# One ring of double PSUM banks for scores and products, layer 0's v bias moved to ScalarE, token sums in two bursts

## The chip, the cores and the metric

The kernel runs on one core of a Trainium2 chip. The metric is the device time of one execution in microseconds; the kernel before has a median of 4040.7 us over three runs (4039.68 to 4045.5). Five engines work side by side, each in its own order of instructions: TensorE (PE in the profile; its weight loads are shown apart as PEld), VectorE (DVE), ScalarE (ACT), GpSimd (POOL) and SyncE (SP, which issues DMA). TensorE writes its products to PSUM[...], from where ScalarE or VectorE must read them before the bank can be used again.

## The reference

Two attention layers over x of shape (4, 32, 32, 768): 4 images, 1024 tokens each, 768 channels. Each layer adds its result to its input:

```python
x = x + _L0_conv_ref(_gn(x), Wq, bq, Wk, bk, Wv, bv, Wp, bp, rel_h, rel_w)
x = x + _L1_conv_ref(_gn(x), w_qkv, b_qkv, w_pool_q, ..., w_proj, b_proj)
```

_gn normalizes over 32 groups of channels. Layer 0 is attention with 12 heads of 64 channels and decomposed relative positions:

```python
q, k, v = heads(x @ Wq + bq), heads(x @ Wk + bk), heads(x @ Wv + bv)
attn = einsum('bqd,bkd->bqk', q, k) / sqrt(64)
attn = softmax(attn + rel_bias_h[:, :, :, :, None] + rel_bias_w[:, :, :, None, :])
return (attn @ v) @ Wp + bp
```

Layer 1 does the same after a depthwise 3x3 convolution and a layer norm over the 64 channels of a head on each of q, k and v, and adds its q to the attention's result before the projection.

The rows of a softmax sum to one, so the v bias bv of layer 0 may be added after the weighted sum: attn @ (x Wv + bv) = attn @ (x Wv) + bv. It may also be moved behind the projection, as the constant bv @ Wp + bp.

## The kernel before

**Work.** The kernel goes through 8 stages (an image and a layer; two images at a time), each of 6 pairs of heads: 48 pairs. A pair has 1024 queries in 2 chunks of 512 (QC) and 8 tiles of 128 keys (NKT).

**Attention of a pair (attend).** For a chunk, 2 groups of 4 key tiles. A score tile is 128 keys x 512 queries for both heads of the pair, in 2 PSUM banks: q times k for each head (line 669), and the position bias, added by a product with a matrix of ones (line 671). ScalarE takes the exponential of both banks into the tile e (line 676), VectorE adds e into acc (lines 682, 684), and TensorE multiplies v with e into the bank av (line 690). After the last group ScalarE copies av (line 632). The sums of the softmax follow while the next chunk is under way: a product of acc with ones into the bank z (sums, line 639), logarithm and exponential on ScalarE as a reciprocal, one Newton step and the product on VectorE (result, lines 654 to 661). These late parts are taken out of the list `rest`, one at each of four places of a chunk (more).

**The other products.** While a pair attends, TensorE makes the next pair's q, k and v. In layer 1: six products (padded, "qkv"), three centrings for the layer norm (centre, "ln_c", two banks each), four transposes back (back, "ln_t"). In layer 0, after the first two pairs, a Strassen scheme with seven products of quarters (sevens): first half into the banks m4m2 and m3m5, second half into m1m6 and m7. It works on sums of quarters of the tokens, which mix_tokens makes with five VectorE instructions (line 234) for each stage. In both layers: products with the position tables (positions, "rel", 2 banks one after the other), from which ScalarE, VectorE and a DMA by GpSimd make the bias (split, line 544). Finally each stage is projected (project, line 723), 12 products for a stage, laid beside the first pair of a later stage.

**PSUM.** Three pools: ps_s, two score tiles of 2 banks each; ps_av, 1 bank; ps_m, a ring of three single banks for all other products. A tile of a pool goes to the place of the tile that many places before it, and its first matmul waits until that tile's readers are done.

**Layer 0's v bias.** In the first image of each layer, project makes the product of the projection's weights and the v bias for each of 6 output blocks (pbias, lines 709 to 714; in layer 1 it is the layer norm's bias), adds the projection's bias and keeps it for all images. The projection's eviction on VectorE (line 723) adds it.

**Order.** The order on TensorE, VectorE, ScalarE and GpSimd is written out by hand: attend yields 16 steps for each pair, and the dictionary `events` says which pieces are emitted at each step. Of 16 steps, a group of four score tiles comes before steps 0, 4, 8 and 12, and the value products of the group before steps 2, 6, 10 and 14. For the stage that follows a layer 1 stage, the quarters' sums come at steps 0 to 4 of the pair before it, and the first Strassen product at step 4.

Of the kernel before, what the change touches and what calls it, by code (L numbers as in the profile page):

```python
# [9 lines left out]
F32 = mybir.dt.float32  # L10
F32R = mybir.dt.float32r
I32 = mybir.dt.int32
AF = mybir.ActivationFunctionType
ALU = mybir.AluOpType
AX = mybir.AxisListType
PSUM = bass.MemoryType.PSUM
# [29 lines left out]
def two_layers(ctx: ExitStack, tc: tile.TileContext, keep, x_in, wqkv, wproj, rels, windows, vrow, small, const, onehot, picks, out):  # L46
# [25 lines left out]
    work = pool("work", 2)  # L72
    one = pool("one", 1)
    stat = pool("stat", 3)
    ps_s = pool("ps_s", 2, space=PSUM)
    ps_av = pool("ps_av", 1, space=PSUM)
    ps_m = pool("ps_m", 3, space=PSUM)

    def bank(name):
        return ps_m.tile([P, 512], F32, tag="bank", name=name)  # L80

    def halves(ps, a, b, start=True, stop=True, **kw):

# [17 lines left out]
    def col(c, lo=0, hi=P):  # L101
        return sm[lo:hi, c : c + 1]
# [134 lines left out]
    def group_norm(stage):  # L237

        xn = xns[stage]
        st = stat.tile([P, NC * 2, 6], F32, tag="bn", name="bn", bufs=1)  # L240
        for n in range(NC):
            for h in range(2):
                nc.vector.bn_stats(st[:, 2 * n + h, :], xn[:, n, h * HALF : (h + 1) * HALF])
            if n in (1, 3):
                yield
        mv = stat.tile([P, 2], F32, tag="mv", name="mv")
        nc.vector.bn_aggr(mv, st.rearrange("p a b -> p (a b)"))
        yield
        yield
        group = cst[:, GROUP : GROUP + P]  # L250
        ps = bank("gn_mean")
        nc.tensor.matmul(ps[:, 0:1], group, mv[:, 0:1], start=True, stop=True)
        mean = stat.tile([P, 1], F32, tag="gmean", name="gmean")
        nc.vector.tensor_copy(mean, ps[:, 0:1])
        d = stat.tile([P, 1], F32, tag="gd", name="gd")
        nc.vector.tensor_sub(d, mv[:, 0:1], mean)
        nc.vector.scalar_tensor_tensor(d, d, d, mv[:, 1:2], ALU.mult, ALU.add)
        yield
        yield
        ps = bank("gn_var")  # L260
        nc.tensor.matmul(ps[:, 0:1], group, d, start=True, stop=True)
        v = stat.tile([P, 1], F32, tag="gv", name="gv")
        nc.vector.tensor_scalar(v, ps[:, 0:1], EPS, None, ALU.add)
        yield
        r = rsqrt(v, 1, "gn")
        yield
        for n in range(NC):
            nc.vector.tensor_scalar(xn[:, n, :], xn[:, n, :], mean, r, ALU.subtract, ALU.mult)  # L268
            if n % 2:
                yield  # L270
# [7 lines left out]
    sk = fixed.tile([P, NSMALL], F32, tag="sk", name="sk")  # L278
    nc.vector.tensor_scalar(sk, sm, SCALE, None, ALU.mult)

    pbias = fixed.tile([P, 2, NC], F32, tag="pbias", name="pbias")

    ones = fixed.tile([P, T], F32R, tag="ones", name="ones")
    plain = one.tile([P, T], F32, tag="whole", name="plain")
# [8 lines left out]
    class Pair:  # L293
# [15 lines left out]
        def sevens(self, s, second):  # L309

            xn = xns[self.b, self.layer]
            x11, x12, x21, x22 = (xn[:, n : n + 3, h : h + HALF] for n in (0, 3) for h in (0, HALF))

            def m(ps, at, x, more=False):

                w = weights[self.i, s, at // 2][:, 3 * (at % 2) : 3 * (at % 2) + 3, :]  # L320
                for t in range(4 if s else 1):
                    for n in range(3):
                        flags = dict(start=not (t or n or more), stop=n == 2, skip_group_check=True)
                        if s:
                            tokens = slice(t * P, (t + 1) * P)
                            halves(ps[:, tokens], x[:, n, tokens], w[:, n, :], **flags)
                        else:
                            halves(ps, w[:, n, :], x[:, n, :], **flags)

            add = lambda to, x, y, op=ALU.add: nc.vector.tensor_tensor(to, x, y, op)  # L330
            u, w = terms
            if not second:
                self.banks = b1, b2 = bank("m4m2"), bank("m3m5")
                m(b1, 0, x21)
                nc.scalar.copy(u, b1)
                m(b2, 1, x12)
                used((self.i, s, 0))
                add(u, u, b2)
                m(b1, 2, x11, more=True)
                add(w, u, b1, ALU.subtract)  # L340
                self.put(s, 1, 0, b1)
                m(b2, 3, x22, more=True)
                used((self.i, s, 1))
                add(u, u, b2, ALU.subtract)
                self.put(s, 0, 1, b2)
            else:
                b3, b4 = bank("m1m6"), bank("m7")
                m(b3, 4, quarters[0])
                add(u, u, b3)
                m(b4, 5, quarters[2])  # L350
                used((self.i, s, 2))
                self.put(s, 0, 0, b4, u)
                m(b3, 6, quarters[1], more=True)
                used((self.i, s, 3))
                self.put(s, 1, 1, b3, w)
# [258 lines left out]
    def attend(pair, os):  # L614
# [12 lines left out]
        for c in range(T // QC):  # L627
# [6 lines left out]

            def sums(weighed, acc, c=c):

                z = bank("z")
                for j in range(2):
                    nc.tensor.matmul(  # L639
                        z[j * D : (j + 1) * D, :], cst[:, ONES : ONES + D], acc[:, j, :],  # L640
                        start=True, stop=True,
                    )
                at = 2 * (pair.i * (T // QC) + c)
                t = work.tile([P, QC], F32, tag="t", name="t", bufs=1)
                inv = work.tile([P, QC], F32, tag="inv", name="inv", bufs=1)
                nc.scalar.activation(t, z, AF.Copy, accum_out=seen[:, at : at + 1])

                nc.scalar.activation(inv, t, AF.Ln, bias=tiny)
                nc.scalar.activation(inv, inv, AF.Exp, scale=-1.0, accum_out=seen[:, at + 1 : at + 2])
                return weighed, t, inv  # L650

            def result(weighed, t, inv, cols=cols):

                nc.vector.scalar_tensor_tensor(t, t, -1.0, inv, ALU.mult, ALU.mult)
                nc.vector.scalar_tensor_tensor(inv, t, 2.0, inv, ALU.add, ALU.mult)

                if pair.layer:
                    nc.vector.tensor_tensor(inv, weighed, inv, ALU.mult)
                    nc.vector.scalar_tensor_tensor(q[:, cols], inv, col(LN + 4), q[:, cols], ALU.mult, ALU.add)
                else:  # L660
                    nc.vector.tensor_tensor(q[:, cols], weighed, inv, ALU.mult)

            for g in range(0, NKT, 4):
                es = []
                for kt in range(g, g + 4):
                    keys = slice(kt * P, (kt + 1) * P)
                    ps = ps_s.tile([P, 2, QC], F32, tag="s", name="s")
                    for j, rows in enumerate(heads):
                        nc.tensor.matmul(ps[:, j, :], k[rows, keys], q[rows, cols], start=True, stop=False)  # L669
                    for j, rows in enumerate(heads):  # L670
                        nc.tensor.matmul(  # L671
                            ps[:, j, :], ones[rows, keys], bias[c][rows, kt // 2, :],
                            start=False, stop=True,
                        )
                    e = work.tile([P, 2, QC], F32, tag="e", name="e", bufs=4)
                    nc.scalar.activation(e, ps, AF.Exp)  # L676
                    es.append(e)
# [15 lines left out]
                        )  # L693
                more()
                if g + 4 == NKT:
                    rest.extend((sums, result))
                    found = (copy(av), acc)
                yield
                yield
# [1 line left out]
    def project(stage, os):  # L701
# [3 lines left out]
        for m in range(NC):  # L705
            w = wp.tile([P, NC, P], F32, tag="wproj", name="wproj_t")
            nc.sync.dma_start(w, wproj[layer, :, :, m, :].rearrange("h p q -> p h q"))
            bias = col(BIAS[layer] + 18 + m)
            if b == 0:
                ps = bank("pbias")  # L710
                for n in range(NC):
                    v_bias = col(LN + 5) if layer else col(BIAS[0] + 12 + n)
                    nc.tensor.matmul(ps[:, 0:1], w[:, n, :], v_bias, start=(n == 0), stop=(n == NC - 1))
                nc.vector.tensor_tensor(pbias[:, layer, m : m + 1], ps[:, 0:1], bias, ALU.add)
            bias = pbias[:, layer, m : m + 1]
            for h in range(2):
                cols = slice(h * HALF, (h + 1) * HALF)
                x = wp.tile([P, HALF], F32, tag="x", name="x")
# [11 lines left out]
    def at(step, piece):  # L730
        events.setdefault(step, []).append(piece)
# [3 lines left out]
    for k in range(1, len(stages)):  # L735
# [5 lines left out]
        if stages[k][1] == 0:  # L741
            mix = mix_tokens(stages[k])
            for r in range(5):
                at(first + 5 * n_steps + r - (0 if stages[k - 1][1] else 8), lambda mix=mix: next(mix, None))
        elif stages[k - 1][1] == 0:
            at(first + 4 * n_steps + 6, lambda: [nc.gpsimd.memset(pad, 0.0) for pad in pads])
    mix = mix_tokens(stages[0])
# [29 lines left out]
    def check():  # L777
# [2 lines left out]
        nc.vector.tensor_reduce(total, seen, AX.X, ALU.add)  # L780
        good = stat.tile([P, 1], F32, tag="good", name="good")
        nc.vector.tensor_scalar(good, total, LIMIT, None, ALU.is_lt)
        ps = bank("good")
        nc.tensor.matmul(ps[:1, :1], cst[:, ONES : ONES + 1], good, start=True, stop=True)
        bad = keep.tile([1, 1], mybir.dt.int32, tag="bad", name="bad")
        nc.vector.tensor_scalar(bad, ps[:1, :1], -1.0, 1.0 * P, ALU.mult, ALU.add)
# [297 lines left out]
```

## Time and profile before

The profiled execution has a span of 4038.7 us, at a mean granted TensorE clock of 0.996.

| what | number |
|---|---|
| TensorE busy | 3945.2 us, 98% |
| weight loads busy | 1720.3 us, 43% |
| VectorE busy | 2494.3 us, 62% |
| ScalarE busy | 1812.1 us, 45% |
| GpSimd busy | 409.8 us, 10% |
| score matmuls, line 669 | 3072 records, 831.8 us |
| bias matmuls of the scores, line 671 | 1536 records, 615.6 us |
| exponentials, line 676 | 768, 1.023 us each |
| one pair of layer 1 without projection | 76.9 us (1128.21 to 1205.13) |
| VectorE busy in it | 66.4 us |

A matmul of fp32 shows as two records. A row of groups gives the line, engine, operation, what it writes and reads, how often, the busy time and the mean of one; the idle time of the engine just before those instructions comes after the bar. A row of waits reads "engine, what waited <- what it waited for: us in total, times, longest". In a timeline a row is a merged run of equal instructions with its start and its duration; the number after x counts them.

### The profile page before, as it was taken

Reading aid. Unit: us, or ns where it says so; the run is one execution under the profiler, and the core shown is the slowest. Engines: PE = TensorE matmul, PEld = TensorE weight load, DVE = VectorE, ACT = ScalarE, POOL = GpSimd, SP = SyncE. Lnnn points to the kernel's source line nnn. Section 1 sums busy time; section 2 is a strip of 40 time slices with the busy share of each in tenths; the row PEclk is TensorE's granted clock in tenths of the full one; section 3 lists DMA queues with packets and bytes.
Section 4 is the critical chain, followed back from the end, with each engine's and each line's share of the span. In section 5 each row is a group of like instructions: output and inputs, shape, how many; then the busy total and the mean of one; then the engine's idle time right before and its main releaser. Section 6 shows DMA issues by size and latency. Waiting matters only on the chain.

```text
span 4038.7 us, 79929 instructions
## 1 busy us (share of the span) xinstructions
PE 3945.2 (98%) x35098; PEld 1720.3 (43%) x35098; DVE 2494.3 (62%) x2800; ACT 1812.1 (45%) x2669; POOL 409.8 (10%) x776
## 2 busy tenths in 40 slices
PE   7999999999999999999899999999999999999999
PEld 3534444434344444444444344354343444434443
DVE  2455423558489985799633454245575898848883
ACT  2444424545255553455423544244443555525552
POOL 0111100110000110010011110001100011000010
PEclk9999999999999999999999999999999999999999
DMA  5333242221411222212133222422114112131112
GB/s 160 85 112 113 71 128 73 57 65 38 132 48 38 76 52 75 63 49 69 41 103 88 58 70 63 144 58 70 47 53 127 37 43 53 40 104 43 38 47 75
DMA packets 179046, 293.34 MB, mean 73 GB/s; under 512 B 22528, under 2 KB 77952, under 8 KB 178688
## 3 DMA queue, kind: packets, MB, share of 16 engines
q1 hardware_dynamic: 117248, 187.41, 14.8%
q0 software_dynamic: 61440, 100.71, 10.9%
q8 instruction: 279, 4.57, 0.5%
q14 instruction: 79, 0.65, 0.1%
HBM read 153.36 MB, written 34.01 MB: 46 GB/s over the span
## 4 chain that ended last, share of the span: by engine, by line
PE 85%; DVE 8%; ACT 3%; issue 1%; DMA 1%; POOL 0%; DVEq 0%; SPq 0%; ACTq 0%
PE qkv L85 18%; PE av L690 14%; PE s L669 14%; PE proj L85 12%; PE m3m L85 4%; PE m4m L85 4%; PE m1m L85 4%; PE s L671 3%; PE ln_c L85 3%; PE rel L517 3%; PE z L639 2%; DVE shared L459 2%; DVE acc L684 2%; PE m L85 2%; ACT e L676 2%
## 5 line engine op out<-in xcount | busy, mean ns | idle before, releaser
L676 ACT ACTIVATE e<-s 128x1024 f32<-128x1024 f32 x768 | 781.3, 1023 | 529.8 <-PE s L671 503.7
L669 PE MATMUL s<-q,k 64*128 64x512 f32 x3072 | 831.8, 618 | 27.9 <-ACT e L676 22.2
L684 DVE TENSOR_TENSOR acc<-acc,e 128x1024 f32<-128x1024 f32 x576 | 705.4, 1225 | 184.4 <-ACT e L676 133.4
L85 PE MATMUL qkv<-xn,wqkv_t 128*64 128x512 f32 x3648 | 815.6, 596 | 2.8 <-DVE xn L268 2.6
L459 DVE SCALAR_TENSOR_TENSOR shared<-shared,sm 128x1056 f32<-128x1056 f32 x576 | 758.3, 1316 | 14.9
L671 PE MATMUL s<-bias,ones 64*128 64x512 f32 x1536 | 615.6, 794 | 13.9 <-DMA bias<-whole 9.5
L690 PE MATMUL av<-e,vt 128*64 128x512 f32 x2624 | 594.5, 595 | 0.0
L544 POOL DMA_DIRECT2D bias<-high x384 | 204.1, 552 | 3356.5 <-ACT high L533 3097.9
L85 PE MATMUL proj<-q,wproj_t 128*64 128x512 f32 x2304 | 504.9, 593 | 0.0
L85 PEld LDWEIGHTS qkv<-xn,wqkv_t 128*64 128x64 f32 x3648 | 252.9, 137 | 488.5 <-issue 482.6
L669 PEld LDWEIGHTS s<-q,k 64*128 64x128 f32 x3072 | 255.4, 186 | 362.0 <-ACT e L676 210.6
L442 ACT ACTIVATE shared<-qkv,sm 128x512 f32<-128x512 f32 (+1 forms) x288 | 129.2, 501 | 595.6 <-PE qkv L85 595.6
L723 DVE SCALAR_TENSOR_TENSOR x<-proj,pbias,x 128x512 f32<-128x512 f32 x96 | 72.1, 751 | 439.4 <-PE proj L85 435.0
L690 PEld LDWEIGHTS av<-e,vt 128*64 128x64 f32 x2624 | 184.7, 137 | 347.5 <-issue 328.9
L682 DVE TENSOR_TENSOR acc<-e 128x1024 f32<-128x1024 f32 x96 | 117.6, 1225 | 345.4 <-ACT e L676 344.6
L85 PEld LDWEIGHTS proj<-q,wproj_t 128*64 128x64 f32 x2304 | 163.7, 137 | 313.5 <-issue 311.7
L671 PEld LDWEIGHTS s<-bias,ones 64*128 64x128 f32 x1536 | 150.2, 188 | 199.6 <-issue 193.6
L544 POOL DMA_DIRECT2D bias<-whole x384 | 204.9, 562 | 119.5 <-DVE whole L534 109.0
L632 ACT COPY weighed<-av 128x512 f32<-128x512 f32 x96 | 56.3, 586 | 329.2 <-PE av L690 329.2
L85 PEld LDWEIGHTS ln_c<-cst,shared 128*64 128x64 f32 x2304 | 131.4, 138 | 44.4 <-issue 34.6
L517 PEld LDWEIGHTS rel<-q,rel 64*32 64x32 f32 x6144 | 111.6, 105 | 78.0 <-issue 61.0
L85 PE MATMUL ln_c<-cst,shared 128*64 128x128 f32 x2304 | 139.2, 274 | 3.1 <-DVE shared L459 3.1
(119 smaller groups left out, 3613.0 us busy)
## 6 DMA issues: line engine op xcount, KB each, us to landing
bias<-high POOLq DMA_DIRECT2D x384, 128.0 KB, 2.8
bias<-whole POOLq DMA_DIRECT2D x384, 128.0 KB, 3.0
wqkv_t<-in_wqkv SPq DMA_DIRECT2D x78, 384.0 KB, 3.1
wqkv_t<-mixed SPq DMA_DIRECT2D x66, 384.0 KB, 3.1
wproj_t<-in_wproj SPq DMA_DIRECT2D x48, 384.0 KB, 3.7
wqkv_t<-in_wqkv SPq DMA_DIRECT2D x66, 192.0 KB, 2.5
xn<-in_x SPq DMA_DIRECT2D x24, 512.0 KB, 7.8
x<-in_x SPq DMA_DIRECT2D x48, 256.0 KB, 2.8
```

What stands on the lines that cost most here:

```text
L85: nc.tensor.matmul(ps[lo : lo + D], a[:, lo : lo + D], b, start=start, stop=stop, **kw)
L442: nc.scalar.activation(self.pad[s][:, rows, there : there + src.shape[2]], src, AF.Identity, bias=col(self.column(s)))
L459: nc.vector.scalar_tensor_tensor(y, window, tap, y, ALU.mult, ALU.add)
L517: nc.tensor.matmul(ps[lo : lo + S, k * S : (k + 1) * S].rearrange("p (b c) -> p b c", b=2), rel[rows, 2 * self.layer + i, first : first + ...
L544: nc.gpsimd.dma_start(sets, some.unsqueeze(1).to_broadcast([D // 2, 2, QC]))
L639: nc.tensor.matmul(z[j * D : (j + 1) * D, :], cst[:, ONES : ONES + D], acc[:, j, :], start=True, stop=True,)
L669: nc.tensor.matmul(ps[:, j, :], k[rows, keys], q[rows, cols], start=True, stop=False)
L671: nc.tensor.matmul(ps[:, j, :], ones[rows, keys], bias[c][rows, kt // 2, :], start=False, stop=True,)
L676: nc.scalar.activation(e, ps, AF.Exp)
L682: nc.vector.tensor_tensor(acc, es[0], es[1], ALU.add)
L684: nc.vector.tensor_tensor(acc, acc, e, ALU.add)
L690: nc.tensor.matmul(av[j * D : (j + 1) * D, :], pair.vt[:, kt, j * D : (j + 1) * D], e[:, j, :], start=(kt == 0), stop=(kt == NKT - 1),)
```

## The change

The change gives the scores a third tile. PSUM becomes one ring of three tiles of 2 banks (ps_two), from which scores and nearly all other products take a tile; a product that needs one bank uses the first half of its tile, and each half of a Strassen step takes the two halves of one tile. One bank remains for av, and one (ps_small) for the small products: z, the group norm's means and variances, pbias, and the last check. To fit these, two other things move. Layer 0's v bias is no longer sent through the projection: ScalarE adds it when it writes the attention's result into q, in a third late part (finish). And in the stage that follows a layer 1 stage, the five quarters' sums come three at step 0 and two at step 1.

```diff
-    ps_s = pool("ps_s", 2, space=PSUM)
+    ps_two = pool("ps_two", 3, space=PSUM)
     ps_av = pool("ps_av", 1, space=PSUM)
-    ps_m = pool("ps_m", 3, space=PSUM)
+    ps_small = pool("ps_small", 1, space=PSUM)
+
+    def banks(name):
+        return ps_two.tile([P, 2, 512], F32, tag="two", name=name)

     def bank(name):
-        return ps_m.tile([P, 512], F32, tag="bank", name=name)
+        return banks(name)[:, 0, :]
+
+    def small_bank(name):
+        return ps_small.tile([P, 512], F32, tag="small", name=name)
...
-                self.banks = b1, b2 = bank("m4m2"), bank("m3m5")
+                two = banks("m4m2_m3m5")
+                b1, b2 = two[:, 0, :], two[:, 1, :]
...
-                b3, b4 = bank("m1m6"), bank("m7")
+                two = banks("m1m6_m7")
+                b3, b4 = two[:, 0, :], two[:, 1, :]
...
-                z = bank("z")
+                z = small_bank("z")
...
                 else:
-                    nc.vector.tensor_tensor(q[:, cols], weighed, inv, ALU.mult)
+                    nc.vector.tensor_tensor(inv, weighed, inv, ALU.mult)
+                return (inv,)
+
+            def finish(inv, cols=cols):
+                if not pair.layer:
+                    nc.scalar.activation(q[:, cols], inv, AF.Identity, bias=col(pair.column(2)))
...
-                    ps = ps_s.tile([P, 2, QC], F32, tag="s", name="s")
+                    ps = banks("s")
...
-                    rest.extend((sums, result))
+                    rest.extend((sums, result, finish))
...
-            if b == 0:
-                ps = bank("pbias")
-                for n in range(NC):
-                    v_bias = col(LN + 5) if layer else col(BIAS[0] + 12 + n)
-                    nc.tensor.matmul(ps[:, 0:1], w[:, n, :], v_bias, start=(n == 0), stop=(n == NC - 1))
-                nc.vector.tensor_tensor(pbias[:, layer, m : m + 1], ps[:, 0:1], bias, ALU.add)
-            bias = pbias[:, layer, m : m + 1]
+            if layer:
+                if b == 0:
+                    ps = small_bank("pbias")
+                    for n in range(NC):
+                        nc.tensor.matmul(ps[:, 0:1], w[:, n, :], col(LN + 5), start=(n == 0), stop=(n == NC - 1))
+                    nc.vector.tensor_tensor(pbias[:, m : m + 1], ps[:, 0:1], bias, ALU.add)
+                bias = pbias[:, m : m + 1]
...
-                at(first + 5 * n_steps + r - (0 if stages[k - 1][1] else 8), lambda mix=mix: next(mix, None))
+                at(first + 5 * n_steps + (r // 3 if stages[k - 1][1] else r - 8), lambda mix=mix: next(mix, None))
```

More of the change, by code (lines that the diff above doesn't have):

```diff
@@ L250, in group_norm @@
         group = cst[:, GROUP : GROUP + P]
-        ps = bank("gn_mean")
+        ps = small_bank("gn_mean")
         nc.tensor.matmul(ps[:, 0:1], group, mv[:, 0:1], start=True, stop=True)
@@ L259, in group_norm @@
         yield
-        ps = bank("gn_var")
+        ps = small_bank("gn_var")
         nc.tensor.matmul(ps[:, 0:1], group, d, start=True, stop=True)
@@ L279, in two_layers @@
     nc.vector.tensor_scalar(sk, sm, SCALE, None, ALU.mult)
-    pbias = fixed.tile([P, 2, NC], F32, tag="pbias", name="pbias")
+    pbias = fixed.tile([P, NC], F32, tag="pbias", name="pbias")
     ones = fixed.tile([P, T], F32R, tag="ones", name="ones")
@@ L782, in check @@
         nc.vector.tensor_scalar(good, total, LIMIT, None, ALU.is_lt)
-        ps = bank("good")
+        ps = small_bank("good")
         nc.tensor.matmul(ps[:1, :1], cst[:, ONES : ONES + 1], good, start=True, stop=True)
```

## Prediction

> **What bounds the kernel now.** I read the busy table first, then the list of waits, then the timeline of one score group on TensorE and on ScalarE.
>
> ```profile
> PE 3945.2 (98%) x35098; PEld 1720.3 (43%) x35098; DVE 2494.3 (62%) x2800; ACT 1812.1 (45%) x2669; POOL 409.8 (10%) x776
> ```
>
> TensorE is the bound: it is idle for 93.5 of 4038.7 us, and no other engine is over 62%. So the change can gain only two things: TensorE instructions that go away, and stalls of TensorE. The waits (who waited on what, us in total, times, longest) name the stalls, and one spare place that is used below:
>
> ```profile
> PEld s L669 <- ACT e L676: 210.6, 383, 2.4
> PE s L669 <- ACT e L676: 22.2, 43, 1.8
> PE s L671 <- DMA bias<-whole: 9.5, 4, 2.9
> ACT weighed L632 <- PE av L690: 329.2, 96, 21.0
> PEld m4m L85 <- DVE xn L234: 7.4, 2, 6.2
> ```
>
> The first line is the one that matters: the weight load of a score tile waits for the exponential, which still reads the buffer that the tile will be written into. Little of it shows as idle matmul time (second line), because the matmuls' ends are modelled and cover it. What it really costs must be read from start times. One group of four score tiles on TensorE (start us, busy us):
>
> ```profile
> 1013.59 1.13 PE L669 MATMUL s<-q,k 64*128 64x512 f32 x4
> 1014.15 0.80 PE L671 MATMUL s<-bias,ones 64*128 64x512 f32 x2
> 1014.78 1.03 PE L669 MATMUL s<-q,k 64*128 64x512 f32 x4
> 1015.23 0.80 PE L671 MATMUL s<-bias,ones 64*128 64x512 f32 x2
> 1016.06 1.13 PE L669 MATMUL s<-q,k 64*128 64x512 f32 x4
> 1016.62 0.80 PE L671 MATMUL s<-bias,ones 64*128 64x512 f32 x2
> 1017.26 1.02 PE L669 MATMUL s<-q,k 64*128 64x512 f32 x4
> 1017.71 0.80 PE L671 MATMUL s<-bias,ones 64*128 64x512 f32 x2
> 1018.45 1.08 PE L639 MATMUL z<-acc,cst 128*64 128x512 f32 x4
> ```
>
> and the same stretch on ScalarE:
>
> ```profile
> 1014.98 2.11 ACT L676 ACTIVATE e<-s 128x1024 f32<-128x1024 f32 x2 [10.63 <-PE s L671]
> 1017.46 2.12 ACT L676 ACTIVATE e<-s 128x1024 f32<-128x1024 f32 x2 [0.36 <-PE s L671]
> ```
>
> The second tile (1014.78) has a free buffer: 0.45 us from its start to its bias matmuls, and after bias matmuls the next tile can follow in 0.63 us (1014.15 to 1014.78). A tile that waits for nothing thus takes 0.45 + 0.63 = 1.08 us. The third tile needs the first one's buffer: the exponential runs from 1014.98 to 1016.0, the tile starts at 1016.06. It follows the second by 1.28 us, and because its weights could not be loaded ahead its own first part takes 0.56 us instead of 0.45, so that the fourth follows by 1.20. Each group loses (1.28 + 1.20) - 2 x 1.08 = 0.31 us.
>
> [...] which the two-bank tiles of the Strassen products need; no trace of before shows two engines inside one such tile.
>
> **The change part by part.**
>
> **1. Third score buffer.** Removed: the stall of the third tile, in all 192 groups (48 head pairs x 2 query chunks x 2 groups). From the start times of all 768 score tiles, the distances from second to third tile add up to 270.0 us (least 1.28; a fifth of them 1.6 or more, where ScalarE began the first exponential late), those from third to fourth to 231.8. At 1.085 us each they would be 208.3 and 208.3, so 61.7 + 23.5 = 85 us can go. The exponential is no new bound: ScalarE does two in 2.11 us, and their starts lie 1.09 apart in the trace, and the fourth tile, at 1.19 + 2 x 1.085 = 3.36 us after the first, needs an exponential that mostly ends at 2.42.
>
> Given back: in three groups the third tile came 3.0 us after the second, since the first exponential was late; there the fourth tile waits instead, some 0.85 us each, 2.6 us. In ten head pairs the first group waits for the DMA of its position bias, and not for a buffer (the third wait above, and its fellows; the 13 such waits have 17.8 us). That DMA starts one to three groups after the products it comes from, so what those groups gain, about 0.6 us, is waited away: 6 us. **Sum: 76 us.**
>
> **2. One ring for all.** Added: scores wait for products' readers and products for exponentials. I put all PSUM tiles of the trace into program order and compared, for each of the 1422 that will share the ring, the end of the last read of the tile three places before with its own first matmul. No tile would have to wait that does not wait now. The least room that is new is 0.73 us (the first score tile after a layer 1 q/k/v product, evicted by ScalarE; 96 tiles, median 1.46), then 0.87 (score tile after a centring product), 1.34 (product after a score) and 1.60 (score tile after a projection, which VectorE evicts). No stall that disappears lies between a product and the first two score tiles after it, so those rooms stay. Four projections keep 0.15, but they have that predecessor now too. Cost 0, with upper bound below. The sums' bank z, alone in its pool, is read by ScalarE long before the next z: 0.
>
> **3. v bias of layer 0.** Removed: the six layer 0 bias products. This row has both layers:
>
> ```profile
> L713 PE MATMUL pbias<-sm,wproj_t x144: 250/250/271, 522.1 to 1626.5; 128*128 128x1 f32 x144
> ```
>
> From the first of 12 such matmuls to the projection after them TensorE spends 1.43 us in every case, on its own path: 6 x 1.43 = **8.6 us**. Added: 48 ScalarE activations of 128x512 from SBUF, 0.72 us each by the q activations of line 410 that also read SBUF; 35 us of ScalarE, off the path. Each is queued behind the fourth exponential of a group. In 46 of 48 places ScalarE's next instruction starts 2.56 us or more after that exponential, since it waits for the value products (the fourth wait above: 3.4 us on average), and VectorE's input was ready 1.2 us or more before. In the other two a layer norm is 0.7 us later. Nothing there is waited for by TensorE: 0. VectorE writes the product to another tile: same instruction, 0.
>
> **4. Quarters' sums.** Once, at 1966.93, TensorE waits for a sum of tokens, 5.5 us. VectorE did the first two from 1957.03, then the four of the result (2.8 us), then the next two. Now five follow one another, the fourth ends at 1957.03 + 4 x 1.755 = 1964.05: 2.8 us sooner. But the four accumulations behind them (5.2 us) end 1.9 us later, and the Strassen step's first VectorE sum is queued behind these, which returns 1.1. **1.7 us.**
>
> Sum 76 + 8.6 + 1.7 = 86 us: 4040.7 - 86 = **3955 us**.
>
> **The rivals.** *Waits move to the fourth tile or to the ring.* For it: ScalarE's 1.09 per exponential is as long as TensorE's 1.085, so a late ScalarE never catches up inside a group, and weights that come late again cost 0.11. If the fourth tile keeps 0.2 us in all groups (38 us), the time is 3993; if the ring makes the 96 tiles with the least room wait 0.4 us each, the same. Against: 0.9 us of room for the fourth tile, 0.73 for the 96.
>
> *Two-bank tiles are guarded as a whole.* Then a Strassen product in one bank waits for the read of the other: in each of 33 products (22 q/k, 11 v) a ScalarE copy 0.59, then VectorE additions of 0.69 four times[...]: 3.9 us, 127 in all; less the gain, 4082, **slower than before**. Against it is one answer of the timeline, where ScalarE writes a part of the tile "shared" while VectorE reads another:
>
> ```profile
> 999.86 1.21 DVE L477 TENSOR_REDUCE lnv<-shared 128x16 f32<-128x1024 f32 x1
> ...
> 999.97 0.90 ACT L442 ACTIVATE shared<-qkv,sm 128x512 f32<-128x512 f32 x2 [4.28 <-PE qkv L85]
> ```
>
> *The stalls were covered.* If TensorE's slots are longer than the starts say, only the 8.6 us and little else remain: 4032. Against: the 1.08 us tile is seen in every group.
>
> **How the numbers follow.** Forecast 0.75; waits move, 0.15; covered, 0.04; guarded as a whole, 0.06. The low end takes nothing given back (85 + 8.6 + 2.8 = 96 us: 3944). The high end takes in the first rival, 3993. Faster 0.92, same 0.02, slower 0.06.
>
> **What would show it.** After: the wait of the score tile's weight load for the exponential falls from 210 us to under 40; tiles of a group start 1.19, 1.085 and 1.085 us apart; 72 bias matmuls; the Strassen rows keep their waits; the first waits for bias grow by some 6 us. Wrong if new waits of scores on lines 442, 473 or 723 appear, or if the fourth tile starts 1.2 us after the third.

## The result, and the profile after

The changed kernel takes 4166.4 us (median of four, 4161.4 to 4168.9), the kernel before 4041.1 on the same chip: a ratio of 1.0307, 95% interval 1.0289 to 1.0324. It is 125 us slower, where 86 us of gain were forecast.

The busy row of the page after:

```profile
PE 3925.6 (94%) x35026; PEld 1729.8 (42%) x35026; DVE 2492.5 (60%) x2794; ACT 1837.0 (44%) x2717; POOL 411.5 (10%) x776
```

TensorE has less work than before (3945.2) and still the span is 120.8 us longer, so it stands idle: 234 us, against 93.5. The list of waits says for what (engine, what waited <- what it waited for: us in total, times, longest):

```profile
PEld m1m_m L93 <- DVE shared L338: 59.6, 33, 6.3
PEld m4m_m3m L93 <- DVE shared L338: 56.5, 33, 4.0
PEld m4m_m3m L93 <- ACT k L429: 52.6, 22, 2.4
PEld m4m_m3m L93 <- ACT shared L344: 44.6, 33, 1.6
...
PEld m1m_m L93 <- DVE shared L371: 36.8, 22, 1.7
...
PEld s L685 <- ACT e L692: 8.5, 11, 1.8
```

Line 93 is the helper that makes the products, lines 338 and 371 are sums on VectorE, line 344 is a copy on ScalarE, line 429 writes k; m4m_m3m is the two-bank tile m4m2_m3m5, since the profile leaves digits out. The last line is the stall that the change was made for: 210.6 us before, 8.5 now. The lines above it are new. In all 33 Strassen products TensorE waits for VectorE and ScalarE, where the kernel before had such waits in a few (of the weight loads of line 85 for the sums of line 330, 4 of m1m and 2 of m3m, 12.6 us together). Both effects can be seen in the timeline. A group of score tiles on TensorE, after:

```profile
1181.96 1.13 PE L685 MATMUL s<-q,k 64*128 64x512 f32 x4
1182.52 0.80 PE L687 MATMUL s<-bias,ones 64*128 64x512 f32 x2
1183.15 1.02 PE L685 MATMUL s<-q,k 64*128 64x512 f32 x4
1183.61 0.80 PE L687 MATMUL s<-bias,ones 64*128 64x512 f32 x2
1184.24 1.03 PE L685 MATMUL s<-q,k 64*128 64x512 f32 x4
1184.70 0.80 PE L687 MATMUL s<-bias,ones 64*128 64x512 f32 x2
1185.33 1.03 PE L685 MATMUL s<-q,k 64*128 64x512 f32 x4
```

Tiles start 1.19, 1.09 and 1.09 us apart (before: 1.19, 1.28, 1.20), and only the first has the 1.13 of a weight load that did not run ahead: its weights begin to load at 1181.96, with its matmuls, and those of the second at 1182.93, 0.22 us ahead of its matmuls. The first half of a Strassen product for q and k, after, on TensorE; the bracket is idle time and what ended it:

```profile
2517.20 2.74 PE L93 MATMUL m4m_m3m<-xn,wqkv_t 128*64 128x512 f32 x12
2520.63 2.80 PE L93 MATMUL m4m_m3m<-xn,wqkv_t 128*64 128x512 f32 x12 [0.69 <-ACT shared L344]
2524.28 2.80 PE L93 MATMUL m4m_m3m<-xn,wqkv_t 128*64 128x512 f32 x12 [0.86 <-DVE shared L338]
2528.59 2.80 PE L93 MATMUL m4m_m3m<-xn,wqkv_t 128*64 128x512 f32 x12 [1.51 <-ACT k L429]
```

and its readers on ScalarE, then on VectorE:

```profile
2519.99 0.59 ACT L344 COPY shared<-m4m_m3m 128x512 f32<-128x512 f32 x1 [0.38 <-PE m4m_m3m L93]
2527.85 0.69 ACT L429 ACTIVATE k<-m4m_m3m,sk 128x512 f32<-128x512 f32 x1 [7.27 <-DVE shared L338]
```

```profile
2523.54 0.69 DVE L338 TENSOR_TENSOR shared<-shared,m4m_m3m 128x512 f32<-128x512 f32 x1 [2.18 <-PE m4m_m3m L93]
2527.12 0.69 DVE L338 TENSOR_TENSOR shared<-shared,m4m_m3m 128x512 f32<-128x512 f32 x1 [2.90 <-PE m4m_m3m L93]
```

Products 1 and 3 go to the first bank of the tile, 2 and 4 to the second. Product 2 starts at 2520.63, when the copy of product 1 has ended (2520.58), though it writes the other bank; product 3 starts at 2524.28, when the sum that reads product 2 has ended (2524.23); product 4 at 2528.59, after both readers of product 3 (2527.81 and 2528.54). TensorE and its readers take turns here instead of working side by side.

I added up, for each kind of product, the time from each TensorE matmul's start to the next one's start, and took the difference of the profiled runs:

| TensorE time, us | before | after less before |
|---|---|---|
| scores | 984.4 | -73.7 |
| bias products | 17.2 | -8.6 |
| Strassen, first halves | 351.8 | +125.1 |
| Strassen, second halves | 266.3 | +74.8 |
| sums z | 89.9 | +1.9 |
| each other kind | | under 0.6 |

The rows add up to 119.5 us, of the 120.8 by which the span is longer. The two larger gains that were forecast are there, 73.7 us for 76 and 8.6 for 8.6; 200 us in the Strassen products, which were costed at nothing, outweigh them.

### The profile page after: what moved, and what is told of

It reads as the page before. It is cut to its first block, busy times and chain, and to the rows that moved or that the text cites. A ratio compares the mean times of both kernels' runs of the same rounds, so it can differ in the third digit from the quotient of the medians.

```text
span 4159.5 us, 80198 instructions
## 1 busy us (share of the span) xinstructions
PE 3925.6 (94%) x35026; PEld 1729.8 (42%) x35026; DVE 2492.5 (60%) x2794; ACT 1837.0 (44%) x2717; POOL 411.5 (10%) x776
## 4 chain that ended last, share of the span: by engine, by line
PE 86%; DVE 9%; DMA 1%; ACT 1%; issue 1%; POOL 0%; DVEq 0%; SPq 0%; ACTq 0%
PE qkv L93 18%; PE s L685 15%; PE av L706 14%; PE proj L93 12%; PE m4m_m3m L93 9%; PE m1m_m L93 6%; PE s L687 4%; PE ln_c L93 3%; PE rel L527 3%; PE z L649 2%; DVE shared L469 2%; DVE acc L700 2%; DVE shared L338 2%; PE ln_t L505 1%; DMA mixed<-mix 1%
## 5 line engine op out<-in xcount | busy, mean ns | idle before, releaser
L685 PE MATMUL s<-q,k 64*128 64x512 f32 x3072 | 813.9, 605 | 4.9 <-ACT e L692 3.5
L685 PEld LDWEIGHTS s<-q,k 64*128 64x128 f32 x3072 | 283.8, 187 | 257.4 <-issue 216.1
L93 PE MATMUL m4m_m3m<-xn,wqkv_t 128*64 128x512 f32 x1056 | 247.8, 604 | 75.2 <-ACT k L429 33.2
L338 DVE TENSOR_TENSOR shared<-shared,m4m_m3m 128x512 f32<-128x512 f32 x99 | 68.1, 687 | 297.0 <-PE m4m_m3m L93 297.0
L93 PE MATMUL m1m_m<-shared,wqkv_t 128*64 128x512 f32 x792 | 186.5, 607 | 46.2 <-DVE shared L338 28.8
L93 PEld LDWEIGHTS m4m_m3m<-xn,wqkv_t 128*64 128x64 f32 x1056 | 70.7, 138 | 248.6 <-issue 117.4
```

Of the source, the lines that this page charges most:

```text
L93: nc.tensor.matmul(ps[lo : lo + D], a[:, lo : lo + D], b, start=start, stop=stop, **kw)
```

## The experiments

Theory A: a PSUM tile of two banks is guarded as a whole: the waits that the program is given are for the tile and not for its parts, so that every product in one bank waits for the readers of the other. Theory B: one ring of three places is too short for scores and products together.

**Separate tiles.** The changed kernel, with one edit:

```diff
-                two = banks("m4m2_m3m5")
-                b1, b2 = two[:, 0, :], two[:, 1, :]
+                b1, b2 = bank("m4m2"), bank("m3m5")
...
-                two = banks("m1m6_m7")
-                b3, b4 = two[:, 0, :], two[:, 1, :]
+                b3, b4 = bank("m1m6"), bank("m7")
```

> The changed kernel with the Strassen banks taken as four tiles of the ring, one bank of each used, in place of two tiles of two banks; all else as changed. Theory A (a two-bank PSUM tile is guarded as a whole, so that each Strassen product waits for the reader of the other bank): the guard's 200 us go, the time is 3955 to 3970 us, the first Strassen half of q and k takes 10.3 us again (14.0 in the changed kernel) and the second 7.8 (9.8). Theory B (the shared ring is short of places, and products and scores wait for each other): now two more places are taken in each Strassen half, so the time is 4166 us or more.

3963.7 us (3961.7 to 3964.7, five runs), ratio to before 0.9802 (0.9788 to 0.9815). The kernel before took 4043.9 us in the same round, and 4043.3 in the round of the runs with the guard in the first half, the sums and the earlier bias. The same four products on TensorE:

```profile
2374.32 2.75 PE L93 MATMUL m4m<-xn,wqkv_t 128*64 128x512 f32 x12
2376.89 2.75 PE L93 MATMUL m3m<-xn,wqkv_t 128*64 128x512 f32 x12
2379.47 2.75 PE L93 MATMUL m4m<-xn,wqkv_t 128*64 128x512 f32 x12
2382.05 2.75 PE L93 MATMUL m3m<-xn,wqkv_t 128*64 128x512 f32 x12
```

and the first reader on ScalarE:

```profile
2377.11 0.59 ACT L343 COPY shared<-m4m 128x512 f32<-128x512 f32 x1 [0.38 <-PE m4m L93]
```

Product 2 starts at 2376.89, before the copy of product 1 does, and a product follows every 2.58 us. The first half takes 10.30 us, the second 7.82 (medians of q and k; after: 14.02 and 9.85). B falls: the Strassen halves take twice the places of the ring, and the scores hardly wait for their readers (32 waits for VectorE of 0.2 us at most, four for ScalarE of 0.8 at most); the scores as a whole take 72.1 us less than before.

**The guard alone.** The kernel before, with nothing changed but the tiles of the Strassen products, which take two banks from the scores' pool:

```diff
-                self.banks = b1, b2 = bank("m4m2"), bank("m3m5")
+                two = ps_s.tile([P, 2, QC], F32, tag="s", name="m4m2_m3m5")
+                b1, b2 = two[:, 0, :], two[:, 1, :]
...
-                b3, b4 = bank("m1m6"), bank("m7")
+                two = ps_s.tile([P, 2, QC], F32, tag="s", name="m1m6_m7")
+                b3, b4 = two[:, 0, :], two[:, 1, :]
```

> The kernel before, with one edit: each Strassen half takes both its banks as one two-bank tile of the scores' pool. Scores keep two buffers, products keep their ring of three. Theory A: the guard alone costs 33 times (3.7 + 2.0) us and what VectorE's queue adds, 190 to 210 us: 4230 to 4255 us. Theory B: no shared ring for the other products, so no more than a few waits of scores for the Strassen tiles: 4035 to 4070 us.

4244.2 us, ratio 1.0497 (1.0481 to 1.0513): 200 us more than before. From its list of waits:

```profile
PEld s L671 <- ACT e L678: 210.7, 384, 2.4
...
PEld m4m_m3m L85 <- DVE shared L330: 54.2, 33, 3.5
PEld m4m_m3m L85 <- ACT k L421: 52.6, 22, 2.4
PEld m4m_m3m L85 <- ACT shared L336: 45.1, 33, 2.1
```

The scores keep their old stall of 210 us, and the Strassen waits are those of the changed kernel. By kinds of products its first halves grow by 121.8 us and its second by 80.1; no other kind differs by 0.7. So the guard alone makes the whole loss, without the ring.

**The guard in the first half only.** The changed kernel, with b3 and b4 as separate tiles.

> The changed kernel with two-bank tiles for the first Strassen half only (products m4, m2, m3, m5); the second half's two banks are separate tiles of the ring. Theory A (the guard of a two-bank tile costs at each change between its banks): the first halves take 14.0 us, the second 7.8, so 33 x 3.7 = 122 us come back: 4080 to 4095 us. Rival (the loss comes from some other effect of the changed kernel that needs both halves, such as the ring's order): close to 3964 or to 4166 us.

4085.9 us, ratio 1.0110 (1.0095 to 1.0126): 122 us above the run with separate tiles, and the first halves hold 122.8 us more than before, the second 1.4 less. The loss stands in the half that has the two-bank tile, and only there.

**The ring alone.** Separate tiles, the v bias through the projection and the quarters' sums as before.

> The ring of three double tiles and the small bank alone, with separate Strassen tiles; layer 0's v bias goes through the projection as before, and the quarters' sums come as before. Theory A: the third score buffer brings what the prediction gave it, 70 to 80 us: 3960 to 3972 us, and 8 to 10 us above the run with separate tiles and all other edits. Theory B: no faster than before, 4040 us or more.

3975.6 us, ratio 0.9831 (0.9817 to 0.9844): 68 us less than before and 11.9 above the run with separate tiles, so both a little worse than expected. Most pairs are 1.2 to 1.7 us shorter.

**The v bias alone.** The kernel before, with the third late part (finish) and no bias product for layer 0.

> The kernel before with layer 0's v bias added by ScalarE when q is written, and no bias product for layer 0; nothing else. The prediction's working: 8.6 us of TensorE go and nothing is added on its path, 4032 us. Rival: the activation between exponentials holds ScalarE up, so that score tiles wait and the gain is gone, 4038 us or more.

4032.7 us, ratio 0.9974 (0.9963 to 0.9985), 11 us less with an interval of 6 to 15. In the trace the bias products have 8.6 us less; the wait of the scores for the exponential is as before (210.6 us), so there is no sign that the 48 activations of 0.71 us delay a score tile. The scores take 3.5 us more in this one trace, mostly in three groups (of pairs 5, 23 and 29) that begin with a wait for their bias.

**The quarters' sums.** Separate tiles, with the sums at five steps.

> The kernel with separate Strassen tiles, but the quarters' sums at five steps as before. The prediction's working: 1.7 us slower than with separate tiles and sums in two bursts, 3965 us, too little for the clock to tell; in the trace the Strassen product after the last layer 1 pair starts 5 to 6 us after the scores before it, against some 3 us with the bursts. Rival (the bursts hold up VectorE's accumulations and return all): no difference in when the Strassen step ends.

3963.5 us, ratio 0.9809 (0.9795 to 0.9822): no difference that can be told. In the trace the Strassen product starts after an idle stretch of 5.88 us here, and of 3.04 with the bursts, which then lose part of it: their fourth product waits 0.54 us for VectorE. From the last score tile to the last Strassen matmul it is 29.5 us here and 27.4 with the bursts.

**An earlier bias.** The gain of the ring is smaller than the 85 us of stall. I thought that the waits for the bias DMA swallow the rest, and moved the bias forward in layer 0:

```diff
-                    (6, lambda: self.positions(0)),
-                    (8, lambda: self.positions(1)),
-                    (10, lambda: self.split()),
+                    (5, lambda: self.positions(0)),
+                    (6, lambda: self.positions(1)),
+                    (7, lambda: self.split()),
```

> The kernel with separate Strassen tiles, and in layer 0's Strassen pairs the products with the position tables at steps 5 and 6 and the bias at step 7, in place of 6, 8 and 10, so that the bias is there before the next pair's scores. Theory (part of the expected gain is waited away at the bias DMA, in pairs 3, 5, 9, 27, 29, 33): the waits in these pairs, 7.9 us together, and what gain they swallowed, go: 3953 to 3959 us. Rival (the swallowed time is elsewhere): 3963 us.

3967.5 us, ratio 0.9814 (0.9800 to 0.9827): no faster. The waits of the bias matmuls for their DMA do fall, from 20.6 to 10.3 us. But with separate tiles alone the waits hold

```profile
PEld s L683 <- ACT e L690: 9.1, 12, 1.8
```

and with the earlier bias

```profile
PEld s L683 <- ACT e L690: 28.5, 29, 1.8
```

The reason is on ScalarE. In one group whose fourth tile waits now, the first exponential with separate tiles alone starts at 635.24, behind two copies of position products (lines 530, 531). With the earlier bias the same copies are there, and one more instruction of `split` behind them:

```profile
635.12 1.05 ACT L541 CAST high<-whole 128x1024 fp32r<-128x1024 f32 x1
636.20 1.94 ACT L690 ACTIVATE e<-s 128x1024 f32<-128x1024 f32 x2
```

In 18 groups this cast stands ahead of the first exponential, and the fourth score tile comes 1.6 to 2.0 us after the third, where it came after 1.09 with separate tiles alone. The edit thus put a new wait in place of those that it took away. My theory on the rest of the gain isn't borne out by the clock, and this run can't rule it out either.

## Why the prediction was wrong, step by step

**Third score buffer: right.** 76 us were forecast, net; TensorE's time in scores fell by 73.7, and the ring alone brought 68. The distances inside a group are the forecast 1.19, 1.09, 1.09, and the weight load's wait is 8.5 us where "under 40" was written. The terms of what is given back were mis-sized both ways. The waits for the bias were to grow by 6 us and grew by 2 to 4 (17.7 before, 19.6 after, 21.4 with the ring alone). The fourth tiles were to lose 2.6 us; with the ring alone the distances from third to fourth tile add up to 216.3 us, 8.0 over the 208.3 of tiles that wait for nothing (after: 214.4). In the three groups that were foreseen the fourth tile comes 2.41 us after the third, a loss of 1.3 us each and not 0.85, and five more groups lose 0.1 to 1.1 us each. What else lies between 76 and 68 stays open. That the third tile's banks had to come from the products' was not shown: the pools of every kernel run here take eight banks (2 x 2 + 1 + 3 before, 3 x 2 + 1 + 1 after), and none tried more.

**One ring for all: right as to the ring.** A sign of being wrong that the prediction named does appear, score tiles that wait for the projection's reader (line 739 after, line 723 before):

```profile
PEld s L685 <- DVE x L739: 4.0, 17, 0.2
```

But none of these waits is over 0.2 us, and no kind of product in the ring, Strassen apart, takes 0.6 us more than before. With separate tiles, which need more places than the change does, the Strassen waits are gone too. Comparing each last read with the start of the matmul three places later was a sound test of that.

**v bias: right.** 8.6 us forecast, 8.6 in the trace.

**Quarters' sums: right in kind.** 1.7 us forecast, 2.1 in the trace of one run each, nothing on the clock.

**The step that failed** is in part 2, "One ring for all". Its cost of 0 counts waits for a place of the ring, and nothing for putting two products with readers on other engines into one tile. The runs show 200 us there: a product in one bank waits for the readers of the other bank, at each of the five changes of a Strassen product. I had named this as the rival "two-bank tiles are guarded as a whole" and gave it 0.06. That rested on a timeline in which ScalarE writes one part of the tile "shared" (from 999.97 on) while VectorE reads another (999.86 to 1001.07). That tile lies in SBUF. The two rows show that these parts of an SBUF tile are guarded apart, and say nothing on PSUM tiles. Nor does it decide the matter that two engines can work in two banks at one time, which they do with separate tiles: there product 2 is written from 2376.89 on, while ScalarE reads product 1 out of another bank from 2377.11 to 2377.70. It is the program of the changed kernel that makes product 2 wait for ScalarE's copy of product 1; in the program with separate tiles that wait is absent. I could have seen that no trace of before had a PSUM tile with two engines at work in it, wrote so, and still took the cheap end of that unknown as all but certain.

**The rival's size was off too**: 127 us forecast, 200 measured, 6.1 us for each Strassen product instead of 3.9. In the timeline above, the changes of bank cost 0.86, 1.03 and 1.68 us over the usual 0.43 from start to start, and those of the second half 0.96 each: 5.5 us. Of my 3.9 us the reads were 3.35 (0.59 + 4 x 0.69); the rest, for the passing from engine to engine, was an estimate with no trace behind it. In that timeline a reader begins 0.65 us after the last matmul's start (2519.34 to 2519.99), and the next matmul 0.05 after the reader's end: beside the read itself, 0.27 us over the usual distance for each change. And at the third change two readers of one bank come one after the other, VectorE to 2527.81 and ScalarE to 2528.54. Each product that waited is itself some 0.05 us longer (rows of 2.80 and not 2.74 us), which makes 5.7 us, the difference of the medians. The remaining 0.4 us for each product is mostly where VectorE came late with its sum, up to 6.3 us in the waits.

## What to carry to other kernels

Putting two accumulators into one PSUM tile is an edit with a cost of its own: here each change of bank waited for the other bank's reader, 200 us in 33 Strassen products, which turned a gain of 80 us into a loss of 125. Where a ring needs equal places, take two places and leave half of each unused: that version, at 3963.7 us, beats both kernels. And when no trace shows a construct, evidence from its nearest relative (another memory, another tile) proves little: give the bad end its weight, or find a row that shows the very thing.

## What the runs showed of the hardware

A stall of a score tile costs more than the wait itself. Before, 189 of the 192 third tiles take 0.56 us for their first part, and 190 of the second and of the fourth tiles 0.45 (after, 189 of the third tiles take 0.45 too). The second tile's weights begin to load at 1014.55, 0.23 us ahead of its matmuls at 1014.78; those of the third, which waits, at 1016.06, together with its matmuls. So a third buffer brought 0.31 us in a typical group of four, of which 0.20 was waiting.

A free buffer alone does not make weights load ahead, as the prediction's "has a free buffer: 0.45 us" suggests. The first tile of each group follows other products and takes 0.56 us in 180 of 192 groups before and 179 after, also where ScalarE had long been idle (10.63 us in the stretch shown); its weights load together with its matmuls in all 192 groups before and 189 after. The 0.45 holds for a tile that follows another score tile and does not wait.

A product's result is read later than I had expected: after, in the 22 first halves for q and k, ScalarE's copy starts 0.63 to 0.65 us after the last matmul's start, where the next matmul could start after 0.43.
